# A gated attention block on one Trainium2 core: the first batch's opening by halves, biases as columns, constant rows by DMA

## The chip, the core and the metric

The kernel runs on one core of a Trainium2 chip. The core has a matrix engine (PE, with its weight loads shown apart as PEld), a vector engine (DVE), a scalar engine (ACT), a general engine (POOL) and SP, which here only issues DMAs. ACT issues DMAs too. Each engine takes its instructions in the order in which the program holds them, a DMA's issue among them[...]. The time is that of one execution on the device, in microseconds (us). A measured time is the median of several runs.

## What is computed

x has 8 batches of 1024 tokens with 256 channels. Cut to what matters:

```python
xn = _layernorm(x)
qkv = einsum('btc,cd->btd', xn, W_attn) + b_attn     # q, k, v; 16 heads of 16
q, k = _apply_rope(q), _apply_rope(k)                # indexed by head, see below
att = softmax(where(causal, q @ k.T / 4, -inf))
s = (att @ v) @ W_proj + b_proj
gate, up = xn @ wg.T, xn @ wu.T                      # weights are integers times 1/127
g = silu((silu(gate) * up) @ wd.T)
return x + s * g
```

`_apply_rope` takes its positions from axis 1 of an array that is already ordered by head, so the turn depends on the head and not on the token. It can therefore be applied to the weights of q and k and to their biases, once, instead of to q and k themselves. The kernel does so: it turns pairs of neighbouring columns of the q/k weights with a cosine and a sine.

## The kernel before, in words

**Setup.** `xs` holds the tokens of one batch (128 partitions, 8 tiles, 256 channels), `xnT` the normalised tokens transposed, in two halves of 512 tokens and two chunks of 128 channels. Under the heading of the pool `setup` (L855 on) the kernel issues the loads. SP's queue gets both halves of x, the q/k weights `raw`, and the three integer weights `wgi`, `wui`, `wdi`. ACT's queue gets the cosines and sines `cs`, the row of q/k biases `raw_bias`, and `wv`, `bv`, `wp`, `bp`. In the built program the completion of DMAs is counted by eight semaphores, which are dealt in turn to the DMAs of both queues; a DMA waits on its issuing engine until the DMA before it on the same semaphore has landed.

**Constant rows.** `q_st` and `k_st` are the operands of the score matmuls: 64 rows of high and low parts of q and k for four heads, and below them (from row `PARTS`) three rows for a shift, which are 0 in `q_st` and -1 in `k_st` until a shift is written. There are two sets of them, each in two halves. `set_rows` (L196) writes the constants with memsets: for the first set in the setup, one half on DVE and one on POOL, for the second set on POOL at the start of `forward` (L787). `vs` is v with a column of ones for each head; it is filled with ones whole, the first copy on DVE (L874), the second on POOL (L789).

**Norm.** `norm_steps` (L94) returns the steps for one batch: bn_stats and bn_aggr for each of eight tiles (L103, L104), an inverse square root by an integer start and three Newton steps (L110 to L118), and a scale of each tile (L133). For the first batch all of it runs on DVE, ahead of everything else there.

**The turn of the weights.** `turn` (L883) takes a half n of the heads and writes turned weights into `wqk_sb`: three operations on the even columns, three on the odd ones. For n = 0 DVE takes the even ones, for n = 1 POOL takes both. The row of biases is turned the same way on POOL, on one partition, and then brought into columns by four small matmuls into `pb` (L911) and a copy to `bqk_sb` (L912).

**Opening.** `opening.open()` transposes `xs` by PE into PSUM, copied to `xnT` by ACT (L225, L226): four groups, two for each half of the tokens. Then come four projections (`project_qk`, L228): for each half of the tokens one of q and one of k. Each is two matmuls of 512 columns, a copy `high` with the bias on ACT (L246), and the rest `low` on DVE (L249, put off to the next `flush`). SP stores both to DRAM (L254), and `early.load` (L483) fetches them back, rearranged, into `q_st` and `k_st`. The two PSUM buffers named `fill` are shared by the transposes, the projections and v, so each takes the buffer that the one before the last has freed. Behind the second, third and fourth projection stands one reduction over an integer weight each, on DVE (L921); then come two pairs of v (`project_v`) and the casts of the integer weights on ACT (L935). The largest integer is turned into a flag (L945), every engine loads it (L946) and branches: `forward` with exact split weights, or a general one.

**After the branch.** `forward` computes the maxima of the first group's scores (`maxima`, L504 on PE, L513 and L515 on DVE) with the rest of the first batch's projections between them, and then the loop over batches. From there on a list of pieces with assumed costs is dealt to the steps of the attention.

Of the kernel before, what the change touches and what calls it, by code (L numbers as in the profile page):

```python
# [35 lines left out]
def gated_block_kernel(ctx: ExitStack, tc: tile.TileContext, x, wqk, wv, bv, wp, bp, wg, wu, wd, rope, out):  # L36
# [48 lines left out]
    def load_x(b):  # L85
        for half in range(2):
            nc.sync.dma_start(
                out=xs[:, ts(half, QT), :], in_=x[b, ts(half, HALF), :].rearrange("(t p) d -> p t d", p=P)
            )


    scaled = {}

    def norm_steps(b):  # L94


        stats = {}

        def one(t):
            if t == 0:  # L100
                stats["mv"] = small.tile([P, NT, 2], F32, tag="mv", name=f"mv_{b}")
            st = small.tile([P, 6], F32, tag="st", name=f"st_{b}_{t}")
            nc.vector.bn_stats(out=st, in_=xs[:, t, :])  # L103
            nc.vector.bn_aggr(out=stats["mv"][:, t, :], in_=st)  # L104

        def first():

            var, rstd, t = (small.tile([P, NT], F32, tag=tag, name=f"{tag}_{b}") for tag in ("var", "rstd", "newton"))
            stats["root"] = var, rstd, t
            nc.vector.tensor_scalar(var, stats["mv"][:, :, 1], LN_EPS, None, ALU.add)  # L110
            nc.vector.tensor_scalar(rstd.bitcast(I32), var.bitcast(I32), -0.5, float(0x5F3759DF), ALU.mult, ALU.add)

        def step():
            var, rstd, t = stats["root"]
            if b == 0:
                nc.vector.tensor_tensor(t, rstd, rstd, ALU.mult)
                nc.vector.scalar_tensor_tensor(t, t, -0.5, var, ALU.mult, ALU.mult)
                nc.vector.scalar_tensor_tensor(rstd, t, 1.5, rstd, ALU.add, ALU.mult)  # L118
                return
            nc.gpsimd.tensor_tensor(t, rstd, rstd, ALU.mult)  # L120
            nc.gpsimd.tensor_tensor(t, t, var, ALU.mult)
            nc.gpsimd.tensor_scalar(t, t, -0.5, 1.5, ALU.mult, ALU.add)
            nc.gpsimd.tensor_tensor(rstd, rstd, t, ALU.mult)

        def offset():
            _, rstd, t = stats["root"]
            nc.gpsimd.tensor_tensor(t, stats["mv"][:, :, 0], rstd, ALU.mult)
            nc.gpsimd.tensor_scalar(t, t, -1.0, None, ALU.mult)

        def scale(i):  # L130
            _, rstd, t = stats["root"]
            if b == 0:
                nc.vector.tensor_scalar(  # L133
                    xs[:, i, :], xs[:, i, :], stats["mv"][:, i, 0:1], rstd[:, i : i + 1], ALU.subtract, ALU.mult
                )
            else:
                nc.scalar.activation(
                    xs[:, i, :], xs[:, i, :], AF.Identity, bias=t[:, i : i + 1], scale=rstd[:, i : i + 1]
                )
            scaled[b] = i + 1  # L140

        tiles = range(NT)
        return [
            *[lambda t=t: one(t) for t in tiles],
            *[first, step, step, step],
            *([offset] if b else []),
            *[lambda t=t: scale(t) for t in tiles],
        ]

# [17 lines left out]
    one = const.tile([1, 1], F32, name="one")  # L167
    nc.gpsimd.memset(one, 1.0)
# [27 lines left out]
    def set_rows(engine, i, half):  # L196
        q_st, k_st = stacks[i]
        engine.memset(q_st[half][PARTS:, :, :].bitcast(F32), 0.0)
        engine.memset(k_st[half][PARTS:, :, :].bitcast(F32), -1.0)
# [523 lines left out]
    def forward(exact, general=None):  # L723
# [63 lines left out]
        for half in range(2):  # L787
            set_rows(nc.gpsimd, 1, half)
        nc.gpsimd.memset(vs[1], 1.0)  # L789
# [65 lines left out]
    with tc.tile_pool(name="setup", bufs=1) as sp:  # L855

        raw = pe.tile([P, CC, QK], F32, tag="e", name="raw")
        raw_bias = sp.tile([1, 1, QK], F32, name="raw_bias")
        cs = sp.tile([P, 2, QK // 2], F32, name="cs")
        load_x(0)  # L860
        nc.scalar.dma_start(out=cs, in_=rope.partition_broadcast(P))
        nc.scalar.dma_start(out=raw_bias[:, 0, :], in_=wqk[C : C + 1])
        nc.sync.dma_start(out=raw, in_=wqk[:C].rearrange("(c p) n -> p c n", p=P))
        nc.scalar.dma_start(out=wv_sb, in_=wv.rearrange("(c p) n -> p c n", p=P))
        nc.scalar.dma_start(out=bv_sb, in_=bv.partition_broadcast(P))
# [5 lines left out]
        nc.scalar.dma_start(out=wp_sb, in_=wp.rearrange("(c p) n -> p c n", p=P))  # L871
        nc.scalar.dma_start(out=bp_sb, in_=bp.partition_broadcast(P))
        set_rows(nc.vector, 0, 0)
        nc.vector.memset(vs[0], 1.0)  # L874
        set_rows(nc.gpsimd, 0, 1)
        for work in norm_steps(0):
            work()
# [3 lines left out]
        brow = sp.tile([1, 1, QK], F32, name="brow")  # L881

        def turn(src, dst, n, even, odd):  # L883
            rows, chunks = src.shape[:2]

            src, dst = (
                t.rearrange("p c (w n d two) -> p c w n d two", w=2, n=2, two=2)[:, :, :, n] for t in (src, dst)
            )
            half = QK // 8
            cos, sin = (  # L890
                cs[:rows, i, :]
                .rearrange("p (w n d) -> p w n d", w=2, n=2)[:, None, :, n, :]
                .to_broadcast([rows, chunks, 2, half])
                for i in range(2)
            )
            for engine, i, op in ((even, 0, ALU.subtract), (odd, 1, ALU.add)):
                t = sp.tile([P, CC, 2, half], F32, tag=f"turned_{i}", name=f"turned_{rows}_{n}_{i}")[:rows, :chunks]
                engine.tensor_tensor(dst[:, :, :, :, i], src[:, :, :, :, i], cos, ALU.mult)
                engine.tensor_tensor(t, src[:, :, :, :, 1 - i], sin, ALU.mult)
                engine.tensor_tensor(dst[:, :, :, :, i], dst[:, :, :, :, i], t, op)  # L900

        turn(raw_bias, brow, 0, nc.gpsimd, nc.gpsimd)
        turn(raw, wqk_sb, 0, nc.vector, nc.gpsimd)
        turn(raw_bias, brow, 1, nc.gpsimd, nc.gpsimd)
        turn(raw, wqk_sb, 1, nc.gpsimd, nc.gpsimd)

        pb = fill_tile("pb")

        def biases():
            for i in range(QK // P):  # L910
                nc.tensor.matmul(pb[:, i : i + 1], brow[0:1, 0, ts(i, P)], one, start=True, stop=True)  # L911
            nc.vector.tensor_copy(bqk_sb, pb[:, : QK // P])  # L912

        opening = Batch(0, None)
        for _, piece in opening.open():
            piece()
        biases()
# [8 lines left out]
        for n, (_, piece) in enumerate(sum(qk[:4], [])):  # L926
            piece()
            flush()
            if n % (2 * CC) == 2 * CC - 1:
                for which in range(2):  # L930
                    early.load(which, n // (2 * CC))
            if n % 2 and n > CC:
                reduces.pop(0)()
        for w_sb, wi in ints:
            nc.scalar.copy(w_sb, wi)  # L935
        load_x(1)
        for _, piece in sum(v[:2], []):
            piece()
# [63 lines left out]
```

## Time and profile before

| what | value |
|---|---|
| median of 3 runs | 1583.12 us (1580.37 to 1586.11) |
| the profiled execution | 1587.18 us |
| its span in the profile | 1585.4 us |
| PE busy | 1507.6 us (95%) |
| DVE busy | 1085.5 us (68%) |
| ACT busy | 959.4 us (61%) |
| POOL busy | 740.7 us (47%) |

The span runs from the first to the last recorded instruction; the profiled execution's own time is 1.8 us longer. A busy share is a mean over the whole span and hides the stages. The page cuts the span into 40 slices of 39.6 us and gives each engine's busy share in tenths; for PE these are `4889999...` with a 7 at the end. A chain of waits is followed back from the last instruction, each step to what released it. A wait for several semaphores is put down to the one that came last in the profile. In the page's lists a releaser stands behind an arrow, as in `<-DMA cs<-in_rope`.

Some landmarks of the opening, from the timeline (start of each, us):

| us | engine | what |
|---|---|---|
| 0.8 | SP | first half of x issued |
| 7.6 | DVE | first bn_stats |
| 15.6 | DVE | first scaled tile |
| 16.1 | PE | first transpose |
| 22.9 | PE | first projection |
| 26.3 | ACT | first `high` |
| 30.3 | SP | first load into `q_st` |
| 37.6 | DVE | flag |
| 40.9 | PE | first score matmul for the maxima |

### The profile page before, as it was taken

What the parts mean: (1) busy time and instruction counts of PE and PEld (TensorE: products, weight loads), DVE (VectorE), ACT (ScalarE), POOL (GpSimd) and SP (SyncE); (2) the same over time, 40 slices, a digit from 0 to 9 for tenths busy, and PEclk for the clock granted to TensorE, in tenths of its full rate; (3) what the DMA queues carried; (4) which work ended last, traced back from release to release, by engine and by line L of the source; (5) the groups of instructions that cost most, each with busy time, mean ns of one, the idle gap of its engine ahead of it and who ended that gap; (6) DMA issues with size and microseconds to landing.
All of it is one profiled execution on the core that took longest, in us unless ns stands there. A gap on an engine that the chain in (4) does not pass through costs nothing.

```text
span 1585.4 us, 29513 instructions
## 1 busy us (share of the span) xinstructions
PE 1507.6 (95%) x9801; PEld 1054.3 (66%) x9801; DVE 1085.5 (68%) x3284; ACT 959.4 (61%) x2076; POOL 740.7 (47%) x1443
## 2 busy tenths in 40 slices
PE   4889999999999999999999999999999999999997
PEld 2567667676677766776666766767666676666664
DVE  6876776767767677776667666776676767777742
ACT  2256665576656666566655766657665666656664
POOL 4554443554436443464434734355343544434353
PEclk9999999999999999999999999999999999999999
DMA  6812554334464255543346344444455335445301
GB/s 180 185 29 41 108 106 76 76 55 104 98 104 65 51 106 97 98 75 67 94 77 111 58 95 95 75 94 62 94 108 88 68 49 110 93 75 81 48 15 43
DMA packets 92086, 132.86 MB, mean 84 GB/s; under 512 B 13714, under 2 KB 41874, under 8 KB 91923
## 3 DMA queue, kind: packets, MB, share of 16 engines
q1 hardware_dynamic: 90944, 129.82, 43.4%
q8 instruction: 80, 1.31, 0.4%
q10 hardware_dynamic: 978, 1.05, 0.3%
q14 instruction: 84, 0.68, 0.2%
HBM read 87.82 MB, written 41.94 MB: 82 GB/s over the span
## 4 chain that ended last, share of the span: by engine, by line
PE 85%; DVE 4%; ACT 4%; POOL 2%; issue 2%; DMA 2%; SPq 1%; DVEq 0%; ACTq 0%; POOLq 0%
PE pw L562 20%; PE av L598 17%; PE pm L504 16%; PE ph L325 11%; PE pqk L234 6%; PE pd L379 6%; PE po L432 3%; PE pv L267 3%; ACT e L569 2%; PE py L616 2%; DVE trash L515 1%; DMA qk<-high 1%; PE pxt L225 1%; PE pq L540 1%; DVE low L249 1%
## 5 line engine op out<-in xcount | busy, mean ns | idle before, releaser
L569 ACT ACTIVATE e<-pw 128x512 f32<-128x512 f32 (+2 forms) x1280 | 678.7, 558 | 427.8 <-PE pw L562 396.8
L515 DVE CUSTOM_DVE_ANT_0 trash<-pm,mask_q 128x128 bf16<-128x128 f32 (+3 forms) x1024 | 501.3, 490 | 336.0 <-PE pm L504 297.0
L562 PE MATMUL pw<-q_st,k_st 67*128 67x512 f32 (+3 forms) x1536 | 554.3, 394 | 8.0 <-ACT e L569 5.5
L504 PE MATMUL pm<-k_st,q_st 65*128 65x512 f32 (+3 forms) x1536 | 520.9, 377 | 6.9 <-DMA qk<-high 3.7
L562 PEld LDWEIGHTS pw<-q_st,k_st 67*128 67x128 f32 x1536 | 277.7, 189 | 205.6 <-issue 100.3
L576 POOL TENSOR_SCALAR_AFFINE_SELECT e<-e 128x256 f32<-128x256 f32 x512 | 206.6, 408 | 437.0 <-ACT e L569 435.3
L513 DVE TENSOR_REDUCE top_far<-pm 128x1 f32<-128x512 f32 x512 | 338.6, 684 | 70.3 <-PE pm L504 69.1
L504 PEld LDWEIGHTS pm<-k_st,q_st 65*128 65x128 f32 x1536 | 279.6, 191 | 57.7 <-issue 17.2
L598 PE MATMUL av<-e,v_sb 128*32 128x512 f32 (+3 forms) x3072 | 293.1, 499 | 0.3 <-POOL e L576 0.3
L356 POOL TENSOR_TENSOR th<-th,ups 128x256 f32<-128x256 f32 x192 | 140.5, 732 | 231.5 <-DVE th L352 225.4
L598 PEld LDWEIGHTS av<-e,v_sb 128*32 128x32 f32 x3072 | 81.0, 110 | 133.6 <-issue 100.6
L360 POOL TENSOR_TENSOR h_low<-th,h_high 128x256 fp32r<-128x256 f32 x192 | 140.7, 733 | 15.4
L234 PE MATMUL pqk<-xnT,wqk_sb 128*128 128x512 f32 x256 | 133.9, 609 | 0.3 <-DVE bqk_sb L912 0.3
L325 PE MATMUL ph<-xnT_high,wg_sb 128*128 128x256 f32 x384 | 102.1, 288 | 12.0 <-DVE th L352 9.0
L379 PE MATMUL pd<-wd_sb,h_high 128*128 128x256 f32 x384 | 99.0, 286 | 7.9 <-ACT yT L423 4.7
L352 DVE SCALAR_TENSOR_TENSOR th<-th,ph 128x256 f32<-128x256 f32 x192 | 79.7, 415 | 31.2 <-ACT ups L341 30.8
L325 PE MATMUL ph<-xnT_high,wu_sb 128*128 128x256 f32 x384 | 101.1, 285 | 0.0
L379 PE MATMUL pd<-wd_sb,h_low 128*128 128x256 f32 x384 | 98.3, 285 | 1.7 <-POOL h_low L360 1.7
L325 PE MATMUL ph<-xnT_low,wg_sb 128*128 128x256 f32 x384 | 99.2, 281 | 0.0
L325 PE MATMUL ph<-xnT_low,wu_sb 128*128 128x256 f32 x384 | 99.1, 280 | 0.0
L337 ACT ACTIVATE th<-ph 128x256 f32<-128x256 f32 x192 | 73.7, 384 | 39.3 <-PE ph L325 34.5
L515 DVE DVE_READ_ACCUMULATOR2_ANT top<- 128x1 f32 x1024 | 85.0, 83 | 0.2 <-issue 0.2
(98 smaller groups left out, 1669.6 us busy)
## 6 DMA issues: line engine op xcount, KB each, us to landing
q_st<-qk SPq DMA_DIRECT2D x256, 128.0 KB, 4.1
k_st<-qk SPq DMA_DIRECT2D x256, 128.0 KB, 5.4
qk<-high SPq DMA_DIRECT2D x64, 256.0 KB, 2.9
qk<-low SPq DMA_DIRECT2D x64, 256.0 KB, 2.8
xs<-in_x SPq DMA_DIRECT2D x16, 512.0 KB, 8.3
res<-in_x SPq DMA_DIRECT2D x32, 256.0 KB, 4.9
out<-res SPq DMA_DIRECT2D x32, 256.0 KB, 2.3
q_st<-rows SPq DMA_DIRECT2D x128, 8.0 KB, 2.1
```

The source lines that it names most:

```text
L234: nc.tensor.matmul(pt, wqk_sb[:, c, ts(i, P)], xnT[:, c, ts(half, HALF)], start=(c == 0), stop=(c == CC - 1),)
L325: nc.tensor.matmul(pt, self.weights[up][:, c, ts(hc, P)], part[:, c, ts(quarter, QU)], start=(c == 0 and i == 0), stop=(c == CC - 1 and i ...
L356: nc.gpsimd.tensor_tensor(h, th, ups, ALU.mult)
L360: nc.gpsimd.tensor_tensor(low, th, high.bitcast(F32), ALU.subtract)
L379: nc.tensor.matmul(pt, h[:, ts(i, P)], self.weights[2][:, hc, :], start=(hc == 0 and n == 0), stop=(hc == HC - 1 and n == len(hs) - 1),)
L504: nc.tensor.matmul(pm[:, ts(i, n)], self.q_st[half][:SHIFT, head, at], self.k_st[keys][:SHIFT, head, :n], start=True, stop=True,)
L513: nc.vector.tensor_reduce(self.top_far[:, head, qt - QT : qt - QT + 1], pm, AX.X, ALU.max)
L515: nc.vector.tensor_tensor_reduce(trash[:, :n], pm[:, ts(i, n)], mask_q[:, HALF - n :], 1.0, MASKED, ALU.add, ALU.max, self.top[:, head, qt ...
L562: nc.tensor.matmul(pw[:, ts(i, n)], self.k_st[kb // QT][:, head, ts(kb % QT, P)], self.q_st[half][:, head, lo:], start=True, stop=True,)
L569: nc.scalar.activation(e[:, first : first + count, lo:], pw[:, : count * n].rearrange("p (a n) -> p a n", n=n), AF.Exp,)
L576: nc.gpsimd.affine_select(out=e[:, :, lo : lo + P], in_=e[:, :, lo : lo + P], pattern=[[0, 2], [1, P]], compare_op=ALU.is_ge, fill=0.0, ba ...
L598: nc.tensor.matmul(self.av[ts(j, SLOT), lo:], vs[self.batch.b % 2][:, kb, at : at + SLOT], es[j // 2][:, j % 2, lo:], start=(kb == 0), sto ...
```

## The change

Six things are changed, all in the setup but for the code that they leave out elsewhere.

- **Loads.** SP now issues the first half of x, the q and k weights of the first half of the heads, the second half of x, the other q/k weights, then `wv`, `bv`, the three integer weights, `wp`, `bp`. ACT issues `cs` and the new `bias`.
- **Norm by halves.** `norm_steps` takes a range of tiles; the first batch calls it twice, for four tiles each, with the turn of the first half of the heads between them on DVE. Other batches call it for all eight as before.
- **Biases.** The host lays out the bias as columns, the same with the two members of each pair exchanged, and the matching cosines and signed sines (128 x 16 numbers). POOL multiplies twice and adds once. The turn of the bias row, the four matmuls and the copy are gone.
- **Constant rows.** Two short rows of 0 and -1 (`fills`) are written by POOL, and eight DMAs on ACT's queue repeat them into the rows of both sets. All eight are issued ahead of ACT's first copy of `xnT`.
- **Ones of v.** POOL writes only the columns of ones and the tail, for both copies in the setup.
- **Opening by halves.** Transposes and projections of the first half of the tokens, their loads into `q_st` and `k_st`, then the same for the second half. The first reduction over integer weights follows the second half's last `low`; the other two follow one pair of v each. The load of batch 1 is issued ahead of v.

In the built program the eight fills wait, on ACT, for the landing of the DMAs that had their semaphores before: the first piece of `raw` for q, the last for k, `bv`, `wgi`, the first fill, `wui`, `wdi`, `wp`, in this order.

```diff
-    def set_rows(engine, i, half):
-        q_st, k_st = stacks[i]
-        engine.memset(q_st[half][PARTS:, :, :].bitcast(F32), 0.0)
-        engine.memset(k_st[half][PARTS:, :, :].bitcast(F32), -1.0)
+    FILL = 64
+
+    def set_rows(queue, fills, i, half):
+        for j in range(2):
+            queue.dma_start(
+                out=stacks[i][j][half][PARTS:, :, :].bitcast(F32).rearrange("r h (a f) -> r (h a) f", f=FILL),
+                in_=fills[:, j, None, :].to_broadcast([ROWS - PARTS, 4 * HALF // FILL, FILL]),
+            )
+
+    def set_ones(engine, i):
+        whole = vs[i][:, :, : HEADS * VS].rearrange("p t (h s) -> p t h s", s=VS)
+        engine.memset(whole[:, :, :, HD], 1.0)
+        engine.memset(vs[i][:, :, HEADS * VS :], 0.0)
...
-        for half in range(2):
-            set_rows(nc.gpsimd, 1, half)
-        nc.gpsimd.memset(vs[1], 1.0)
...
-        load_x(0)
         nc.scalar.dma_start(out=cs, in_=rope.partition_broadcast(P))
-        nc.scalar.dma_start(out=raw_bias[:, 0, :], in_=wqk[C : C + 1])
-        nc.sync.dma_start(out=raw, in_=wqk[:C].rearrange("(c p) n -> p c n", p=P))
-        nc.scalar.dma_start(out=wv_sb, in_=wv.rearrange("(c p) n -> p c n", p=P))
-        nc.scalar.dma_start(out=bv_sb, in_=bv.partition_broadcast(P))
+        for n in range(2):
+            load_x(0, [n])
+            for which in range(2):
+                nc.sync.dma_start(out=raws[n, which], in_=halves[n][which])
+        nc.scalar.dma_start(out=bias, in_=bqk)
+        nc.sync.dma_start(out=wv_sb, in_=wv.rearrange("(c p) n -> p c n", p=P))
+        nc.sync.dma_start(out=bv_sb, in_=bv.partition_broadcast(P))
...
-        nc.scalar.dma_start(out=wp_sb, in_=wp.rearrange("(c p) n -> p c n", p=P))
-        nc.scalar.dma_start(out=bp_sb, in_=bp.partition_broadcast(P))
-        set_rows(nc.vector, 0, 0)
-        nc.vector.memset(vs[0], 1.0)
-        set_rows(nc.gpsimd, 0, 1)
-        for work in norm_steps(0):
-            work()
...
+        nc.sync.dma_start(out=wp_sb, in_=wp.rearrange("(c p) n -> p c n", p=P))
+        nc.sync.dma_start(out=bp_sb, in_=bp.partition_broadcast(P))
+        fills = sp.tile([ROWS - PARTS, 2, FILL], F32, name="fills")
+        for j in range(2):
+            nc.gpsimd.memset(fills[:, j], (0.0, -1.0)[j])
+        for i in range(2):
+            set_ones(nc.gpsimd, i)
+            for half in range(2):
+                set_rows(nc.scalar, fills, i, half)
...
+        opening = Batch(0, None)
+        for work in norm_steps(0, range(QT)):
+            work()
         turn(raw, wqk_sb, 0, nc.vector, nc.gpsimd)
-        turn(raw_bias, brow, 1, nc.gpsimd, nc.gpsimd)
+
+        for i in range(2):
+            nc.gpsimd.tensor_tensor(bias[:, i], bias[:, i], bias[:, 2 + i], ALU.mult)
+        nc.gpsimd.tensor_tensor(bqk_sb, bias[:, 0], bias[:, 1], ALU.add)
+        for work in norm_steps(0, range(QT, NT)):
+            work()
         turn(raw, wqk_sb, 1, nc.gpsimd, nc.gpsimd)
...
-        for n, (_, piece) in enumerate(sum(qk[:4], [])):
-            piece()
-            flush()
-            if n % (2 * CC) == 2 * CC - 1:
-                for which in range(2):
-                    early.load(which, n // (2 * CC))
-            if n % 2 and n > CC:
-                reduces.pop(0)()
+        opens = opening.open()
+        for half in range(2):
+            for _, piece in opens[half * CC : (half + 1) * CC] + sum(qk[2 * half : 2 * half + 2], []):
+                piece()
+            flush()
+            for which in range(2):
+                early.load(which, half)
+            if half:
+                reduces.pop(0)()
+        load_x(1)
+        for _, piece in v[0]:
             piece()
+        reduces.pop(0)()
+        for _, piece in v[1]:
+            piece()
+        reduces.pop(0)()
         for w_sb, wi in ints:
             nc.scalar.copy(w_sb, wi)
-        load_x(1)
-        for _, piece in sum(v[:2], []):
-            piece()
```

## The prediction

> **What bounds it now.** I read the page's slices first: PE is busy 95% of the span and at 9 tenths from the fourth of its 40 slices on; only the first three (119 us) and the last are thinner. The change touches nothing after the opening but constants, so its whole worth lies before about 75 us, against 1585. Then the chain of waits over that stretch:
>
> ```profile
> 15.90 2.35 DVE xs L133 x7
> ...
> 19.98 0.45 POOL brow L900
> 20.44 0.42 POOL brow L898
> ...
> 21.86 0.84 PE pb L911 x6
> 22.93 5.41 PE pqk L234 x8
> 28.37 0.70 ACT high L246
> 29.09 0.76 DVE low L249
> 29.87 0.32 SPq L254
> 30.28 0.40 SPq L483
> ...
> 34.07 7.16 DMA qk<-high
> 41.24 0.32 SPq L483
> ...
> 47.69 7.73 DMA qk<-high
> 55.53 0.70 ACT high L246
> ```
>
> The columns are start, length, who. The reader sees four legs. To 22.9 us the norm of all eight tiles and the biases hold back the first projection. To 30.3 the projections run. To 40.9 the group's rows come back from DRAM. Then a store that stands behind other transfers (47.69 to 55.4) keeps `high` from its buffer. From 57 us on the chain is VectorE, from 74 PE, so what is saved or lost up to there passes through whole (my assumption). The timeline gives three facts on which the sum turns:
>
> ```profile
> 5.77 0.33 ACTq L872 DMA_DIRECT2D bp_sb<-in_bp  x1
> ...
> 6.13 1.28 ACT L226 ACT_TABLE_LOAD   x1 [6.13 <-DMA cs<-in_rope]
> ...
> 37.61 0.14 DVE L945 TENSOR_SCALAR flag<-most 1x1 int32<-1x1 f32 x1
> 38.48 1.80 POOL L198 MEMSET q_st<- 3x2048 f32 x1 [12.26 <-DVE flag L945]
> ```
>
> `bp` could not be issued until `cs` had landed (0.79 + 5.0 = 5.8), and ScalarE's table load stood behind it. The built program says why: eight completion semaphores are dealt to the DMAs in turn, whatever their queue, and a DMA waits on its own engine for the one that held its semaphore before. The flag that opens the branch was ready at 37.75 and the engines moved 0.75 later, yet the first `pm` began only at 40.91, when `k_st` landed.
>
> **The change, step by step.** *VectorE.* Three memsets (1.76 + 1.76 + 1.97) leave its front, so its first bn_stats moves from 7.6 to the landing of the first half of x. That now shares the queues with `cs` alone: 768 KB at 128, then 314 GB/s (rows 2 to 4 and 4 to 6 us) is through at 5.6, landed near 6.6. Four tiles: stats 4 x 0.53, root 3.64, scale 4 x 0.34, q/k turn 1.2: done by 15.0 instead of 19.4. The root is done twice; the second (about 5.7 us with its stats and scales, ending near 20.7) lies under the waits below. *Biases.* 12 POOL rows of 0.45, four matmuls and a copy go; three small POOL multiplies come at about 10, hidden by the wait for the tokens. PE would be free at 15.1, 7.8 us earlier. The POOL memsets behind the branch (38.5 to 47.5) go too: `xnT_low` follows them, first read at 65, so nothing is gained.
>
> *The rows by DMA: the wait that takes their place.* ScalarE now issues eight fills ahead of its table load and of the copy of `xnT`. The program makes them wait in turn for raw q, raw k, bv, wgi, an earlier fill, wui, wdi and **wp**. All of these weights go down SP's one queue, wp last but one. So ScalarE stands until wp lands, and behind it everything: copies, projections, stores, loads. When is that? Before, the last weight:
>
> ```profile
> wdi<-in_wd SPq DMA_DIRECT2D x1, 768.0 KB, 10.4
> ```
>
> issued at 9.13, landed at 19.5, as the last of 4.98 MB. Ahead of and with wp the same bytes stand, less bp (128 KB, 0.35 us): 19.2. Then one issue 0.45, table load 1.28, two copies of 0.59 that overlap with PE's start: first pqk at **21.6** against 22.93, a gain of 1.3, not 7.8. If this cover fell, VectorE's turn (15.0) would be late next.
>
> *From there.* PE is cold as before: q 4 x 0.85 = 3.4 (to 25.0), k about 2.55 (to 27.55), high 0.69, low 0.75: 29.1, against 29.84; stores and loads follow 0.75 earlier, `k_st` lands at 40.1. The second half's transposes take the buffer that `low` frees: 0.85, copy 0.6, then pqk to 33.35, last `low` at 34.9 (34.48 before). **Here the change gives back**: the three reductions over the integer weights (pitch 1.66 each), which lay between the lows from 29.76 on, now all stand behind the last one, with one addition of v (0.62) among them: 34.9 + 5.6 = 40.5, flag 1.1 later at 41.7, first `pm` at 42.45, 1.55 later than before. The flag, not `k_st`, ends that wait. VectorE then reaches the point where it had idled 1.76 us for `high` (54.49 to 56.25) at 56.05; the DMA in question lands at 54.65, so the stall is gone: 56.05 against 56.25, **-0.2**.
>
> *The clock.* Between 40.5 and 47.2 the granted clock was half:
>
> ```profile
> 40.00:42.00 2.00, 1.06 (x5) 1.09 (x6) 0.00 (x0) 0.67 (x2) 2.00 (x3) 0.63 1.03 393
> 42.00:44.00 2.00, 2.00 (x6) 1.02 (x5) 1.38 (x9) 0.00 (x0) 2.00 (x3) 0.50 1.01 238
> 44.00:46.00 2.00, 2.00 (x7) 1.42 (x5) 1.64 (x9) 0.00 (x0) 1.94 (x2) 0.50 1.11 141
> 46.00:48.00 2.00, 2.00 (x6) 1.13 (x4) 1.47 (x5) 0.69 (x1) 2.00 (x2) 0.66 1.09 122
> ```
>
> (PE, PEld, DVE, ACT, POOL busy, clock, DMA.) VectorE idled 1.6 us over 42 to 50, and its first result took 1.27, half of it cold: 2.2 us in all. [...] By the trace it was 3.3 us at 23.4 but 6.7 here. [...] I take half of the 2.2 (between nothing and all; -0.2 without it): **-1.1**.
>
> Sum -1.3. The profiled execution took 1587.2 (span 1585.4 and 1.8 around it), so 1585.9; its time lies 4.1 above the median of the three runs, 1583.1, so **1581.8** as a median.
>
> **The unknown: a fill's own price.** No row shows a 256-byte piece. Each fill is 3 partitions x 32 pieces. [...] Nearest row: in xs's stretch, 385 GB/s over 16 engines, 1 KB per 42 ns. From below, by bytes, 32 x 10.5 ns = 0.34 us on each of the three; from above, a piece of 256 B as dear as 1 KB, 1.35 us. Seven fills stand ahead of wp's landing: 2.4 or 9.4 us on those engines. Their share of the loads (303 KB at 22 GB/s from 2.4) ends at 16.1, so wp is through there at 18.5 or 25.5. Were the three as good as the sixteen, nothing. I take the lower end, under 19.2, since the engines moved by bytes in every row of large pieces.
>
> **Rivals.**
> - *The queue drains earlier and PE stays warm.* For: the DMA share falls from full at 16.6, the tail to 19.5 is a few engines; wp is not the last piece. wp at 16.5: pqk 2.7 earlier, clock whole 2.2: -0.2 - 2.7 - 2.2 = -5.1, 1578.0. Against: the same tail must serve wp.
> - *The fills do not hold ScalarE*, so that the order by need works: pqk at 15.1, 6.5 earlier: -0.2 - 6.5 - 1.1 = -7.8, 1575.3. Against: bp's wait above is just this hold.
> - *Slower: the fills choke three engines.* At 1.35 us a fill wp lands at 25.5, pqk at 27.9, 6.3 later: -0.2 + 6.3 - 1.1 = +5.0, 1588.1. It decides from about 1.3 us a fill. For: small pieces[...].
> - *The change does nothing of what it says*: that is nearly my forecast, since halves are only of use if ScalarE is free at 14.
>
> **Chances.** Forecast 0.52, its own range 1578.5 to 1586 (wp 17 to 23.5). Drain and warm 0.31, free 0.07, choke 0.10. A measurement here tells about 0.3% (4.75 us) from no change: faster 0.38, same 0.52, slower 0.10. The range 1576.5 to 1587 leaves out the free case, the choke and a few runs below.
>
> **What would show it.** Right: ScalarE's table load near 20 just behind the last fill's issue, first pqk near 21.6, three reductions in a row behind the last low, `pm` released by the flag at 42 or later, no idle VectorE near 55. Wrong: a table load before 16 (free or drained), a wp that lands after 23 (choke), a granted clock of 1.0 after the branch (warm), or any change of busy time or waits beyond 100 us.

## The result: no change that can be measured, by another route than forecast

| | before | after |
|---|---|---|
| median, measured in turns on one chip | 1585.20 us (14 runs, 1580.37 to 1592.91) | 1585.01 us (14 runs, 1582.08 to 1588.14) |
| ratio after/before | | 0.9994, 95% interval 0.9979 to 1.0010 |
| profiled execution, its span | 1587.18, 1585.4 | 1583.77, 1582.0 |
| first projection (PE) | 22.9 | 25.9 |
| flag (DVE) | 37.6 | 45.7 |
| first score matmul `pm` | 40.9 | 47.0 |
| first `e` of the attention (ACT) | 75.0 | 78.6 |

The forecast was 1581.8, range 1576.5 to 1587.0, no change as the likeliest. The time lies in the range, but two errors cancel in it: the opening became 3.6 us longer, not 1.3 shorter, and the granted clock, higher later on, gave that back. The mechanism of the forecast, the hold on ScalarE, was right; that the time came out unchanged is luck. Its base was off too: the median of three runs was 1583.1, that of fourteen 1585.2.

The chain of waits of the changed kernel, start, length, who:

```profile
10.44 12.70 DMA wp_sb<-in_wp
...
23.16 0.73 ACTq L195
...
23.92 1.28 ACT L230
...
25.22 0.60 ACT xnT L230
...
25.90 6.21 PE pqk L238 x8
```

The reader sees the mechanism that the prediction named: `wp` lands, only then ACT may issue the last fill (ACTq L195), then comes its table load, then the copy of `xnT`, then PE. The place is as forecast, the hour is not: `wp` landed at 23.14 instead of 19.2. The timeline of ACT shows the last fills one by one:

```profile
17.22 0.73 ACTq L195 DMA_DIRECT2D q_st<-fills  x1
17.99 0.73 ACTq L195 DMA_DIRECT2D k_st<-fills  x1
20.95 0.73 ACTq L195 DMA_DIRECT2D q_st<-fills  x1
23.16 0.73 ACTq L195 DMA_DIRECT2D k_st<-fills  x1
23.92 1.28 ACT L230 ACT_TABLE_LOAD   x1 [23.92 <-DMA k_st<-fills]
```

Fills seven and eight each stand idle for a weight (`wdi`, `wp`). The same stretch by windows (PE, PEld, DVE, ACT, POOL busy, clock, then the DMA share of 16 engines and GB/s):

```profile
16.00:18.00 2.00, 0.00 (x0) 0.00 (x0) 1.83 (x9) 0.00 (x0) 1.92 (x4) 1.00 1.11 331
18.00:20.00 2.00, 0.00 (x0) 0.00 (x0) 1.81 (x6) 0.00 (x0) 1.30 (x2) 1.00 0.46 130
20.00:22.00 2.00, 0.00 (x0) 0.00 (x0) 1.85 (x8) 0.00 (x0) 0.00 (x0) 1.00 0.33 40
22.00:24.00 2.00, 0.00 (x0) 0.00 (x0) 0.18 (x1) 0.08 (x1) 0.00 (x0) 1.00 0.27 15
```

From 18 us on the 16 engines are busy for less than half the time (0.46, then 0.33); a share of 0.27 is some four engines' time, and it moves 15 GB/s. PE is idle throughout. This is the picture of the "choke", the rival that had a chance of 0.10.

Further on, VectorE's timeline:

```profile
38.95 1.74 DVE L921 TENSOR_REDUCE most<-wgi 128x1 f32<-128x1536 int32 x1
40.61 1.74 DVE L921 TENSOR_REDUCE most<-wui 128x1 f32<-128x1536 int32 x1
42.87 1.74 DVE L921 TENSOR_REDUCE most<-wdi 128x1 f32<-128x1536 int32 x1
45.67 0.14 DVE L950 TENSOR_SCALAR flag<-most 1x1 int32<-1x1 f32 x1
```

All three reductions stand behind the last `low`, with one addition of v between the second and the third, as forecast. And the idle stretch of VectorE near 55 us has gone:

```profile
58.69 1.28 DVE L517 TENSOR_REDUCE top_far<-pm 128x1 f32<-128x512 f32 x2
59.89 0.74 DVE L253 SCALAR_TENSOR_TENSOR low<-pqk,bqk_sb,high 128x512 fp32r<-128x512 f32 x1
60.55 1.28 DVE L517 TENSOR_REDUCE top_far<-pm 128x1 f32<-128x512 f32 x2
```

No bracket stands behind the `low`, so it waited for nothing. Before:

```profile
53.20 1.28 DVE L513 TENSOR_REDUCE top_far<-pm 128x1 f32<-128x512 f32 x2
56.25 0.75 DVE L249 SCALAR_TENSOR_TENSOR low<-pqk,bqk_sb,high 128x512 fp32r<-128x512 f32 x1 [1.76 <-ACT high L246]
56.91 1.28 DVE L513 TENSOR_REDUCE top_far<-pm 128x1 f32<-128x512 f32 x2
```

The first `top_far` began at 53.2 and the third at 56.9; now it is 58.7 and 60.5. The lag of 6.1 us at `pm` is 5.5 at the first `top_far` and 3.6 from the third on. At the end of the span the changed kernel's profiled execution is nevertheless 3.4 shorter. No busy time beyond 100 us explains that; the granted clock does, as the next section shows.

### The profile page after: what moved, and what is told of

Its sections match the earlier page's. It is cut to its first block, busy times and chain, and to the rows that moved or that the text cites. A ratio compares the mean times of both kernels' runs of the same rounds, so it can differ in the third digit from the quotient of the medians.

```text
span 1582.0 us, 29513 instructions
## 1 busy us (share of the span) xinstructions
PE 1500.0 (95%) x9793; PEld 1050.1 (66%) x9793; DVE 1082.7 (68%) x3291; ACT 959.8 (61%) x2076; POOL 723.9 (46%) x1432
## 4 chain that ended last, share of the span: by engine, by line
PE 86%; ACT 4%; DVE 4%; DMA 2%; issue 2%; POOL 1%; SPq 0%; ACTq 0%; DVEq 0%; POOLq 0%
PE pw L566 20%; PE av L602 17%; PE pm L508 16%; PE ph L329 11%; PE pqk L238 6%; PE pd L383 6%; PE po L436 3%; PE pv L271 3%; ACT e L573 2%; PE py L620 2%; DVE trash L519 1%; DMA wp_sb<-in_wp 1%; PE pxt L229 1%; PE pq L544 1%; DVE low L253 1%
## 5 line engine op out<-in xcount | busy, mean ns | idle before, releaser
L602 PE MATMUL av<-e,v_sb 128*32 128x512 f32 (+3 forms) x3072 | 289.3, 494 | 0.3 <-POOL e L580 0.3
```

The source lines that it names most:

```text
L602: nc.tensor.matmul(self.av[ts(j, SLOT), lo:], vs[self.batch.b % 2][:, kb, at : at + SLOT], es[j // 2][:, j % 2, lo:], start=(kb == 0), sto ...
```

## The experiments

Each run leaves the core's mean granted clock, and times are compared at like clock as well as by medians. The runs were taken on three occasions, each with its own runs of the kernel before (medians 1586.44, 1587.01 and 1585.45), and a ratio is to those.

### The same two kernels again: what repeats

The kernel before and the changed kernel, unaltered; two further profiles of the first and two of the second, one execution each.

> The kernel before once more, for a second profile. In the first one PE's clock fell to half for five stretches beside the opening's two or three (from 88, 119, 1068 and 1259 us, each worth about 1.5 us), in the profile after only from 123. Theory A[...]: they lie elsewhere or are fewer here, while all starts up to the first e activation at 75.0 us repeat to within 0.5 us. Rival B (they belong to the schedule before, and the change took them away): dips again near 88, 1068 and 1259 us.

> The changed kernel once more, for a second profile. If the landing of wp holds ScalarE: table load again near 23.9 us, first projection near 25.9, first pm near 47.0, first e activation near 78.6 (3.6 later than before's 75.0). A (luck of the clock): dips elsewhere than in the first profile. B (the change took them away): none beyond 125 us again.

> The kernel before once more, for the places where its clock is half. Over many runs its mean granted clock spread from 0.982 to 0.995 and its time from 1595.7 to 1579.9, 1.2 us for each thousandth; the changed kernel's runs lay at 0.993 to 0.995. Theory (chance: any thin stretch of PE, one in each batch, may fall to half clock for 3.4 us): the half-clock stretches beyond 125 us lie at the thin stretches near 305, 495, 684, 874, 1063 or 1254, in another pick than the two seen, about one for each thousandth that the clock lies under 0.995. Rival (a stretch of the opening, the stall near 55 to 57 above all): they lie before 90 us, where the changed kernel has none.

> The changed kernel once more, for its half-clock stretches. Theory (chance at the thin stretches, more seldom than before, since its runs lie at a mean clock of 0.993 to 0.995): one stretch near 44 behind the branch, one or two near 88 to 123, none to one beyond 125. The opening as in the two profiles seen: table load 23.5 to 24, first projection 25.5 to 26, first e 78.3 to 78.7. Rival (the opening of the profiled runs is not that of the other runs): table load or first e off by over 1.

Measured (us; "half clock" is the length of each stretch that the trace records at half clock, the one at the very end left out):

| profile | first pqk | first e | 41st e | half clock to 80 | 80 to 126 | beyond | time |
|---|---|---|---|---|---|---|---|
| before | 22.93 | 74.99 | 130.0 | 3.4 + 6.8 | 3.4 + 6.8 | 3.4 + 3.4 | 1587.18 |
| rep_before | 23.48 | 76.19 | 128.1 | 6.8 | 3.4 | none | 1581.66 |
| rep_before2 | 22.54 | 73.41 | 129.5 | 3.4 + 6.8 | 6.8 + 6.8 | 3.4 + 3.4 | 1586.39 |
| after | 25.90 | 78.63 | 130.7 | 6.8 | 3.4 | none | 1583.77 |
| rep_after | 25.56 | 78.33 | 130.3 | 10.2 | 3.4 | 3.4 | 1584.78 |
| rep_after2 | 25.75 | 78.23 | 130.3 | 10.2 | 3.4 | 3.4 | 1584.64 |

In the changed kernel the opening repeats; in the kernel before the first `e` ranges from 73.4 to 76.2, wider than the 0.5 expected. In the mean of three profiles it comes 3.5 later (78.4 against 74.9). The half clock beyond 126 us does not repeat: the kernel before had it at 1068 and 1259, then nowhere, then at 689 and 880; the changed kernel nowhere, at 500, at 879. These are places where PE is thin once in each batch (in the first profile 2.67 of 4.00 us busy from 1064 to 1068). From ACT's 41st `e` (the table's fourth column) to the end of the span the nine profiles without such a fall, of these kernels and of those below, take 1450.6 to 1451.8 us, three with one fall 1452.6 to 1453.1, and two with two 1455.1 and 1455.5: a fall, one stretch of 3.4 us, costs some 1.6 to 2. So the times beyond 126 differ by how many of the thin places fall, and not by an instruction of the change. A rival reading, that the falls sit in the stall near 55, is wrong: no profile of the kernel before shows one there. In the clock's record of the first profile of the kernel before, half clock begins at 23.46 and then 5, 19, 28, 306 and 362 times 3.413 us later, and lasts 3.413 or 6.827 us each time (that at the very end left out); in that of the changed kernel it begins at 44.63 and 23 times 3.413 us later, and lasts 6.827 and 3.413 us. What sets this step is not shown.

The clock's record has a gap. In the changed kernel's first projections a matmul starts 0.85 us after the one before it, as at half clock (in the kernel before weight loads at 24.32, 25.17 and 26.02, with the record at 0.50), while the record says 1.00; later the distance is 0.43 (weight loads at 35.22, 35.65 and 36.08):

```profile
28.00:30.00 2.00, 2.00 (x3) 0.75 (x3) 0.00 (x0) 0.24 (x1) 0.00 (x0) 1.00 0.00 0
28.59 0.34 PEld L238 LDWEIGHTS pqk<-xnT,wqk_sb 128*128 128x128 f32 x1 [0.52 <-issue]
29.45 0.34 PEld L238 LDWEIGHTS pqk<-xnT,wqk_sb 128*128 128x128 f32 x1 [0.52 <-issue]
```

This lasts 5.2, 4.2 and 3.5 us in its three profiles. In the kernel before it is on record in two of three (the 3.4 us near 23). So the recorded mean clock flatters the changed kernel, by an estimated 0.001 against the kernel before (half of 4.3 us in 1583 is 0.0014; before it is missing in one profile of three).

Part of the balance does repeat. Between 80 and 126 us the kernel before spends 10.2, 3.4 and 13.6 us at half clock and the changed kernel 3.4 each time, so the lag of 3.5 at the first `e` is 1.2 at the 41st. Windows of the kernel before, then of the changed kernel (columns as above):

```profile
88.00:90.00 2.00, 2.00 (x16) 0.35 (x8) 0.74 (x3) 0.00 (x0) 0.00 (x0) 0.58 0.00 0
90.00:92.00 2.00, 2.00 (x13) 1.81 (x10) 0.64 (x2) 0.39 (x1) 0.41 (x1) 0.57 0.00 0
```

```profile
92.00:94.00 2.00, 2.00 (x20) 1.21 (x13) 0.74 (x4) 0.39 (x1) 0.20 (x1) 1.00 0.00 0
94.00:96.00 2.00, 2.00 (x15) 1.87 (x14) 1.71 (x7) 0.55 (x2) 0.85 (x4) 1.00 0.11 40
```

It is the same place in the work, 4 us apart in time, behind a thin stretch of PE (0.38 of 2.00 us busy from 84 to 86 before, 0.50 from 88 to 90 in the changed kernel). The clock is 0.58 in the one and 1.00 in the other. Over many runs: the 113 runs of the kernel before (111 in turns with others, two profiled alone) have a mean clock of 0.982 to 0.995, mean 0.9901, and cost 1.2 us for each thousandth (a line fitted through them); the 16 of the changed kernel lie at 0.993 to 0.995, mean 0.9939. At 0.994 and 0.995 the kernel before took 1581.2 (mean of 19 runs) and the changed one 1584.4 (9 runs): 3.2 longer, about what its opening says. That is rough: the clock is given to a thousandth, and 17 of the 19 lie at 0.994, six of the nine at 0.995. The mean difference of clock, 0.0038, is worth 4.5 us at that slope, of which the gap in the record makes an estimated 1; the rest is enough to give back what the opening lost. Why the changed kernel's thin stretches fall less often is not settled: the work of these stretches is the same in both, the other kernels below have each a spread of their own, and no run isolates it.

### The hold on ScalarE: constant rows by memset, or by another queue

e_memset writes the rows with memsets again, all on POOL: the first set ahead of its turn of the weights, the second behind the branch.

```diff
-    def set_rows(queue, fills, i, half):
...
+    def set_rows(engine, i, half):
+        q_st, k_st = stacks[i]
+        engine.memset(q_st[half][PARTS:, :, :].bitcast(F32), 0.0)
+        engine.memset(k_st[half][PARTS:, :, :].bitcast(F32), -1.0)
...
+        for half in range(2):
+            set_rows(nc.gpsimd, 0, half)
```

> The changed kernel with the constant rows by POOL memsets as before: the first set ahead of POOL's turn, the second behind the branch. Nothing then stands before ScalarE's table load. Theory 1 (the eight fills hold ScalarE until wp lands): table load near 2, first projection near 15.7 instead of 25.9, first pm near 37 instead of 47.0, first e activation near 68 to 69 instead of 78.6, wp landed by 19.5 instead of 23.1, time 6 to 10 us under the changed kernel, so near 1577 where before is 1585. Rival 2 (the opening has slack behind it, and what is won there is given back by 140 us, as 3.6 fell to 0.7 in the profiles): first pm as above, but the time within 2 us of the changed kernel.

e_sp keeps the eight DMAs, but on SP's queue ahead of `wv`:

```diff
...
+        for i in range(2):
+            for half in range(2):
+                set_rows(nc.sync, fills, i, half)
         nc.sync.dma_start(out=wv_sb, in_=wv.rearrange("(c p) n -> p c n", p=P))
...
-            for half in range(2):
-                set_rows(nc.scalar, fills, i, half)
```

> The changed kernel with the eight fills on SP's queue, ahead of wv, instead of ScalarE's. The small pieces stay, the hold on ScalarE goes; the weights start some 5 us later. Theory 1: first projection near 15.7; the weights land late (wp near 25), so the reductions over the integers wait and the flag comes near 36 to 38; time 4 to 8 us under the changed kernel. If the small pieces themselves are the loss (three engines choked), the first projection still waits or the weights land past 28, and the time is within 2 us of the changed kernel.

Measured, e_memset's ACT:

```profile
1.72 1.28 ACT L228 ACT_TABLE_LOAD   x1 [1.72 <-PEq L996]
```

In both, ACT's table load moved to 1.7 us. First projection at 16.55 (e_memset) and 15.46 (e_sp), against 25.9. e_memset took 1580.19 (22 runs), ratio to before 0.9955 (0.9942 to 0.9968); e_sp 1581.94 (22 runs), 0.9974 (0.9962 to 0.9987). So the order by need does work once ACT is free, and what held it were the fills in ACT's queue: 9.4 us of PE's start are theirs. Of these, 8.3 reach `pm` (38.74 against 47.02) and 7.8 the first `e` (70.86). At a mean clock of 0.994 and 0.995 e_memset took 1576.0 (5 runs) against 1584.4 of the changed kernel (9); by medians the difference is only 4.8, for its runs have a lower mean clock (0.9922). In e_sp the flag came at 39.6, later than the 36 to 38 expected.

e_memset also shows what `wp` takes without fills in any queue. It was issued at 9.89, on the same queue and behind the same loads:

```profile
wp_sb<-in_wp SPq DMA_DIRECT2D x1, 256.0 KB, 9.1
```

It landed at 19.0, about where the prediction had put it with the fills (19.2). So the seven fills ahead of it cost it 4.1 us, 0.6 each.

e_sp shows the price of a fill by itself, for from 10 to 16 us nothing else is in its queues:

```profile
10.00:12.00 2.00, 0.00 (x0) 0.00 (x0) 1.81 (x6) 0.00 (x0) 1.88 (x5) 1.00 0.17 22
12.00:14.00 2.00, 0.68 (x3) 0.45 (x3) 1.84 (x8) 0.00 (x0) 0.00 (x0) 1.00 0.16 18
14.00:16.00 2.00, 2.00 (x8) 1.53 (x8) 1.93 (x7) 0.98 (x2) 0.60 (x1) 1.00 0.16 20
```

A share of 0.16 is the time of 2.6 of 16 engines, and 20 GB/s moved in it: at that rate the 24.6 thousand bytes of one fill take 1.2 us. At three sixteenths of 385 GB/s, the prediction's lower bound, they would have taken 0.34. In e_sp the price falls on the weights behind the fills: SP issues `wv` only at 14.95.

### Is it the number of pieces? Pieces of 2 KB

```diff
-    FILL = 64
+    FILL = 512
```

> The changed kernel with one size altered: a fill is written in pieces of 2 KB (12 of them) instead of 256 B (96), the bytes, the eight DMAs, their queue and their order stay. Theory (the three engines that carry the fills are held up by the number of pieces): wp lands at 19.0 to 20.5 instead of 23.1, ScalarE's table load follows at 19.5 to 21 (23.6 to 23.9 before), the first projection at 21.5 to 23 (25.6 to 25.9), the first score matmul for the maxima near 43.5, and the whole is 2 to 3.5 us under the changed kernel at the same mean granted clock. Rival (wp is late by its place behind all other weights, or by the fills' issue): the table load stays at 23 to 24 and the time as it is, within 1 us at the same clock.

Measured, ACT's timeline:

```profile
21.75 0.73 ACTq L195 DMA_DIRECT2D q_st<-fills  x1
22.53 0.73 ACTq L195 DMA_DIRECT2D k_st<-fills  x1
23.29 1.28 ACT L230 ACT_TABLE_LOAD   x1 [23.29 <-DMA k_st<-fills]
```

An eighth of the pieces, and the table load came only 0.6 earlier. The list of DMA issues (KB, us from issue to landing) gives for `wp`, issued at 10.83:

```profile
wp_sb<-in_wp SPq DMA_DIRECT2D x1, 256.0 KB, 11.7
```

so it landed at 22.5, against 23.1. My theory of the number of pieces fell. The kernel's median was lower all the same, 1582.32 (22 runs), ratio to before 0.9975 (0.9964 to 0.9986), where its profile shows a first `e` only 0.3 earlier. The rest of these 2.7 us is not explained; the mean clock is the same (0.9940), and the intervals of the two ratios overlap.

### Is it the bytes? Half of each fill

The eight DMAs write two of the four heads, in 256-byte pieces as before, and POOL writes the other two.

```diff
-                out=stacks[i][j][half][PARTS:, :, :].bitcast(F32).rearrange("r h (a f) -> r (h a) f", f=FILL),
-                in_=fills[:, j, None, :].to_broadcast([ROWS - PARTS, 4 * HALF // FILL, FILL]),
+                out=stacks[i][j][half][PARTS:, :2, :].bitcast(F32).rearrange("r h (a f) -> r (h a) f", f=FILL),
+                in_=fills[:, j, None, :].to_broadcast([ROWS - PARTS, 2 * HALF // FILL, FILL]),
             )
+            nc.gpsimd.memset(stacks[i][j][half][PARTS:, 2:, :].bitcast(F32), (0.0, -1.0)[j])
```

> The changed kernel with half the bytes in each fill: the eight DMAs, their queue, order and 256-byte pieces stay, but each writes two of the four heads (12 KB), and POOL writes the other two with memsets ahead of its turn. Theory, made after 2 KB pieces had left wp's landing at 22.5 (not the number of pieces, but the bytes that go into three partitions: alone on SP's queue eight fills, 196 KB, took 8.2 to 18.9, about 20 GB/s or 1.2 us each): seven fills at 0.6 instead of 1.2 take 4.2 off, wp lands at 19.5 to 21 instead of 22.5 to 23.1, table load at 20 to 21.8, first projection at 22 to 23.8, time 1.5 to 3.5 under the changed kernel at the same mean granted clock. Rival (the number of DMAs or the place of wp, not their bytes): table load at 23.2 to 24 as before, no gain.

Measured, the chain of waits, and `wp` in the list of issues (issued at 10.66):

```profile
10.22 8.57 DMA wdi<-in_wd
18.82 0.73 ACTq L195
19.58 1.28 ACT L231
20.88 0.60 ACT xnT L231
21.56 6.21 PE pqk L239 x8
```

```profile
wp_sb<-in_wp SPq DMA_DIRECT2D x1, 256.0 KB, 9.9
```

`wp` landed at 20.6 instead of 23.1, 2.6 earlier. This halves the number of pieces too, but an eighth of the pieces had brought only 0.6, so the theory of bytes stands. The table load moved by more, 4.3, because in this build the semaphores are dealt otherwise: the last fill waits for `wdi` (18.79) and not for `wp`, which is worth another 1.8. The median was 1579.97 (8 runs), ratio to before 0.9957 (0.9936 to 0.9978).

This kernel happens to put the first projection at 21.56, where the prediction had put it (21.6). Its place there is chance, but what follows is then a test of the prediction's later steps: flag forecast at 41.7, measured 41.33; first `pm` forecast at 42.45, measured 42.67.

### The give-back: the three reductions

e_reduce puts all three reductions ahead of the opening's loop, where VectorE stands idle.

```diff
+        for reduce in reduces:
+            reduce()
         opens = opening.open()
...
-            if half:
-                reduces.pop(0)()
...
```

> The changed kernel with its three integer reductions ahead of the opening's transposes and projections, where VectorE stands idle, instead of behind the last low; fills and loads as they are. Theory (the reductions behind the last low hold the flag, and the flag holds the branch): reductions near 21 to 27, flag at 40.5 to 41.5 instead of 44.8 to 45.7, first score matmul at 42 to 45.3 (by the landing of the k_st loads near 44.8 if that decides) instead of 46.1 to 47.0; 1 to 3 us under the changed kernel at the same mean granted clock. Rival (the landing of k_st or what follows decides, not the flag): the first e activation moves by less than 0.7 and the time stays.

Measured: reductions from 22.1 on, flag at 41.86 instead of 45.67, but `pm` at 44.37: now the landing of the rows ends that wait, 2.65 earlier. The first `top_far` came 3.0 earlier, and the third only 0.8:

```profile
55.66 1.28 DVE L517 TENSOR_REDUCE top_far<-pm 128x1 f32<-128x512 f32 x2
59.12 0.75 DVE L253 SCALAR_TENSOR_TENSOR low<-pqk,bqk_sb,high 128x512 fp32r<-128x512 f32 x1 [2.18 <-ACT high L250]
59.79 1.28 DVE L517 TENSOR_REDUCE top_far<-pm 128x1 f32<-128x512 f32 x2
```

The old idle stretch is back (2.18, waiting for `high`), and behind it PE fell to half clock for 6.8 us from 61.9. So the first `e` was 1.1 later than in the changed kernel, and the median 1585.23 (14 runs), ratio to before 0.9987 (0.9971 to 1.0004): no gain. `high` waits for its buffer until an earlier store has landed: ACT stood idle 6.15 us for that landing, until 58.40. e_reduce_x, with the early reductions, moves the load of batch 1 (1 MB, first read at 98 us) from ahead of that store to behind the first group's maxima:

```diff
-        load_x(1)
...
         flush()
         first.shift_parts(1)
+        load_x(1)
```

> The kernel with all three reductions early (e_reduce), and the load of batch 1 (1 MB) issued behind the first group's maxima instead of ahead of v. Theory (early reductions brought the first top_far from 58.7 to 55.7, and the wait of high for its buffer, behind a store that shares the queues with that load, took it back and let the clock fall at 62): without the load the store lands earlier, VectorE's idle stretch before the third top_far (57 to 59.8) shrinks by 1.5 to 2.9, the half clock at 62 goes, first e at 75 to 77.5 instead of 79.7, time 2 to 4.5 under e_reduce at the same mean granted clock. Rival (the store stands behind the group's own q and k loads, or SP issues it late): third top_far at 59.5 or later, first e above 79.

```profile
55.63 1.28 DVE L517 TENSOR_REDUCE top_far<-pm 128x1 f32<-128x512 f32 x2
56.83 0.74 DVE L253 SCALAR_TENSOR_TENSOR low<-pqk,bqk_sb,high 128x512 fp32r<-128x512 f32 x1
57.49 1.28 DVE L517 TENSOR_REDUCE top_far<-pm 128x1 f32<-128x512 f32 x2
```

VectorE's wait is gone (ACT's for the store is 2.93 us now), the half clock at 62 with it, and the first `e` is at 75.79, 3.95 earlier than in e_reduce. So the stall is the price of that load in front of the stores (one of them is also issued 0.8 earlier, at 49.84; how much of it is the issue and how much the shared queues is not shown). By medians the two are close, 1584.26 (22 runs; ratio to before 0.9990, 0.9976 to 1.0004) against 1585.23; at a mean clock of 0.994 it is 1583.4 (6 runs) against 1585.0 (4). The expected 2 to 4.5 us were not reached in the time.

### Put together

e_best is e_memset with two reductions behind the first half's lows, where VectorE idled from 24.4 to 28.3, and the third behind the second half's; e_best_x moves the load of batch 1 too.

```diff
-            if half:
+            for _ in range(2 - half):
                 reduces.pop(0)()
...
```

> The kernel with memsets for the constant rows (e_memset), and two of its three reductions behind the first half's lows, where VectorE stood idle from 24.4 to 28.3, the third behind the second half's. Theory (there too the flag ends the wait of the first score matmul): flag near 34 instead of 37.4, first score matmul at 35 to 36.5 instead of 38.7, first e near 68 to 69.5 instead of 70.9, so 1.5 to 3 us under e_memset at the same mean granted clock, and 5 to 6 under the kernel before. Rival (the second half's loads or the half clock behind the branch take it back): first score matmul earlier, first e within 0.7 of 70.9, no gain.

> The fastest kernel so far (memsets, two early reductions) with the load of batch 1 issued behind the first group's maxima. Theory (that load takes queue time from the stores and loads that end the opening): third top_far at 50 to 50.6 instead of 51.2, first e at 67.5 to 68.8 instead of 69.3, 0.5 to 1.8 under e_best at the same mean granted clock. Rival (the load is hidden here, or collides with the next group's loads at its new place): first e within 0.4 of 69.3, or the second group late, and no gain.

| kernel | flag | first pm | first e | median (runs) | ratio to before |
|---|---|---|---|---|---|
| after | 45.67 | 47.02 | 78.63 | 1585.01 (14) | 0.9994 (0.9979 to 1.0010) |
| e_memset | 37.38 | 38.74 | 70.86 | 1580.19 (22) | 0.9955 (0.9942 to 0.9968) |
| e_best | 35.53 | 36.91 | 69.31 | 1575.23 (10) | 0.9945 (0.9922 to 0.9968) |
| e_best_x | 33.91 | 35.73 | 66.83 | 1573.75 (6) | 0.9912 (0.9894 to 0.9930) |

Each step moved the first `e` (by 1.55 and 2.48; for e_best_x 0.5 to 1.8 was expected). The ten runs of e_best lie in two groups, six at 1573.8 to 1575.8 with a mean clock of 0.994 or 0.995 and four at 1579.0 to 1580.6 with 0.990 to 0.992, so its median hangs on how many fall into each; the medians alone would give a ratio of 0.9926. e_best_x beats both kernels; its gain over the kernel before, some 0.9%, is 8.2 us of opening and a higher clock.

## Why the prediction came out as it did, step by step

- **The hold on ScalarE by the weights that lend their semaphores** is shown: the chain runs through `wp`, the last fill and the table load, and without the fills on ACT's queue the table load is at 1.7. The rival that the fills do not hold it fell.
- **VectorE done at 15.0** was near: the first bn_stats came at 7.56 instead of 6.6, and with ACT free the first projection was at 15.5 to 16.6.
- **The landing of wp at 19.2** is the step that failed: 23.1. The term is the price of a fill, and with it the assumption that the seven fills hide behind the loads: without any fill `wp` landed at 19.0 (e_memset), so they cost it 4.1. The prediction had bounds of 0.34 and 1.35 us and took the lower, "since the engines moved by bytes in every row of large pieces". By its own sum (16.1 plus seven fills) 23.1 means 1.0 a fill, three times the value taken; alone on a queue it was 1.2, near its upper bound. But the sum's start is not shown either: 16.1 is when the loads' share of three engines would end, and `wp` landed 2.9 later with no fill at all. It is by bytes (half of them brought `wp` forward by 2.6, an eighth of the pieces by 0.6), but not at the rate of the large rows: with nothing beside them the fills moved 18 to 22 GB/s, where three of the sixteen engines that moved 385 would give 72. That three partitions mean three engines, each at its full rate, was the author's estimate. The traces do not name the engine of a transfer; the fills' share was 0.16 or 0.17 in e_sp (10 to 16 us), the time of 2.6 or 2.7 engines, and 0.24 in the changed kernel (24 to 26 us), that of 3.8, at 20 GB/s in both. What sets that rate is not shown.
- **PE's start** was therefore 25.9 instead of 21.6, 3.0 later than before and not 1.3 earlier.
- **From there to the first pm**, 20.85 forecast, 21.1 measured (20.5 and 20.3 in the two other profiles); in e_half 21.1 likewise. The give-back by the three reductions is shown by e_reduce (flag 3.8 earlier without it), and that the flag ends the wait too: `pm` follows it by 1.35 here and in e_half and e_memset, where before it was 3.3 and waited for `k_st`.
- **The stall near 55 disappears**: right, and worth 1.9 (5.5 of lag became 3.6). e_reduce shows the reason as put: an earlier VectorE meets the stall again.
- **The clock behind the branch, -1.1**: too much. It was an estimate, half of the 2.2 us, and the half clock there lasted 6.8, 10.2 and 10.2 us in three profiles, 6.8 in each one before, so a length beyond the 3.3 and 6.7 that the prediction had read came twice:

```profile
44.00:46.00 2.00, 0.37 (x1) 0.08 (x1) 1.74 (x5) 0.00 (x0) 0.00 (x0) 0.66 1.05 384
46.00:48.00 2.00, 0.98 (x5) 1.02 (x5) 0.00 (x0) 1.21 (x3) 0.51 (x1) 0.50 1.04 204
48.00:50.00 2.00, 2.00 (x6) 1.10 (x5) 1.49 (x9) 0.97 (x2) 2.00 (x3) 0.50 1.10 142
50.00:52.00 2.00, 2.00 (x7) 1.27 (x5) 1.59 (x9) 0.00 (x0) 2.00 (x2) 0.63 1.09 120
```

  The new idle stretch of PE is longer, not shorter (5.9 us without a matmul but the one for the flag, against 4.4), and part of the half clock falls into it. What counts is what is left behind the first `pm`: the clock was whole again 4.4, 7.3 and 7.0 us after it, before 6.4, 6.6 and 7.0. From the first `pm` to the first `top_far` it took 11.7, 12.3 and 12.3 us, before 12.3, 12.3 and 12.1. So the term was worth 0.6 in the profiled execution and nothing in the other two.
- **"What is saved up to 75 us passes through whole"** holds for the work but not for the clock. The prediction knew the clock behind the branch and left out the thin stretches (from 84 to 91, near 120, and once per batch), where a fall costs some 1.6 to 2. They decided the sign of the profiled difference.

Of the signs that the prediction named, the three reductions in a row, the flag as releaser and the missing idle time at 55 came true, the table load near 20 did not, and "a wp that lands after 23 (choke)" did. The rival of a queue that drains early and a warm PE, which had a chance of 0.31, fell with the landing at 23.1 and the half clock behind the branch. The choke's own figure, first projection at 27.9 and 5.0 us lost, was too high: 25.9, and 3.6 at the first `e`.

## What to carry to other kernels

A DMA issue on a computing engine's queue can hold that engine, as here ACT until 23.1 us: find in the built program what it waits for, and what stands behind it. Short constants were cheaper here as memsets on an engine that idled (ratio to before 0.9955 against 0.9994). Where a transfer goes to few partitions, take its rate from such a transfer, not a share of the rate of wide ones, and if the forecast turns on that term, take neither end of its bounds. Where a few microseconds count, compare runs at like mean clock, read how long the half clock lasts before explaining a span, and check the record of the clock by the distance of the matmuls.

## What was not expected of the hardware

- Transfers into three partitions ran at 18 to 22 GB/s together with nothing beside them, with pieces of 256 B; with 2 KB pieces the tail of e_piece took less of the engines' time (a share of 0.10 from 22 to 24 instead of 0.27), but moved 23 GB/s and brought `wp` only 0.6 earlier. What limits them is not shown: no run moved the rows to other partitions, and the source `fills` lies on three partitions too.
- Issuing a fill cost ACT 0.73 us (1.37 for the first), against 0.45 for `cs`.
- The record of the granted clock said 1.00 over a first stretch of 3.5 to 5.2 us in which the matmuls came 0.85 us apart instead of 0.43.
- The mean clock of one unchanged kernel ranged from 0.982 to 0.995 over 113 runs, 1.2 us for each thousandth, a spread of 16 us, three times what was to be measured.
- A change of the fills' shape, with memsets on POOL for the rest, altered which weight the last fill waited for (`wdi` for `wp` in e_half), worth 1.8 us.
